# Row sums of an attention kernel folded onto half of the partitions, and their product with ones moved and halved

## The chip, the core and the metric

The kernel runs on one core of a Trainium2 chip. The metric is the device time of one execution in microseconds (us). Three runs of the kernel before took 2548.26, 2549.02 and 2549.62 us; the median, 2549.02, is the time that the change is measured against. The profiled execution took 2548.74 us, and its span in the profile is 2547.0 us, with a mean granted TensorE clock of 0.995.

## The reference

The input x has four images of 128 channels and 64 x 64 pixels. Layer 0 is a group norm, a 1x1 projection to q, k and v, attention with 4 heads of 32 channels over the 4096 pixels of an image, an output projection and a residual. Layer 1 is two 3x3 convolutions with quantized weights, each with a batch norm, and a residual. Only the attention matters here:

```python
q, k, v = jnp.split(qkv, 3, axis=1)            # (b, 128, 64, 64) each
q, k, v = (to_heads(q), to_heads(k), to_heads(v))   # (b, 4, 4096, 32)
attn = jnp.einsum('bhid,bhjd->bhij', q, k) * scale
attn = jax.nn.softmax(attn, axis=-1)
out = jnp.einsum('bhij,bhjd->bhid', attn, v)
...
out = jnp.einsum('oc,bchw->bohw', proj_w, out) + proj_b[None, :, None, None]
return x + out
```

The softmax's denominator is a sum of exponentials over all 4096 keys for each query and head. This row sum is what the change rearranges.

## The kernel before

**Blocks, steps and halves.** The attention is cut into 32 blocks (4 images x 8 groups of 512 queries), n = 0 to 31. A block runs over 32 key steps (kt) of 128 keys. For each step `scores` makes two matmul groups (`s<-q,k`, two heads each), and ScalarE (ACT) makes the exponentials `p` of both (128 keys on the partitions, 4 heads x 512 queries). `weights` then multiplies p by v into `acc`, in two halves of 256 queries, four matmuls for the four heads in four column bands of the array. There are 64 halves p = 0 to 63 in a block. `run_scores(3)` and `run_weights(3)` alternate, so that the work goes in rounds of three score halves and three weight halves.

**Row sums.** After the second half of a step, p is added into `rsum[n]` by VectorE (DVE, line 471). At the six steps of `MOVED` the addition is done by a DMA instead, into a second tile `msum[n]` (lines 464 and 466); each of these DMAs waits for the one before. Row sums are still split over the 128 partitions (keys), and that last sum is a matmul with a matrix of ones.

**What is left of a block is done in the next one.** `finish_parts(n)` gives closures, and `schedule` puts them at halves of block n+1 (`before[...]`):

- `merge` (half 3): GpSimd's DMA queue (POOL) adds msum into rsum.
- `sums` (line 498): the product with ones, `total`, in two groups of four matmuls of 256 columns, in PSUM tile `l`. Each head's sum comes out 32 times over, once on each partition of the head's band. The two groups come at the ends of two successive rounds, or of one.
- `evacuate`: ACT copies l to `ls`, 512 columns, directly after.
- `spread`, `invert`, `gather`: a DMA spreads the 4 x 512 sums over 128 partitions (`lq`), DVE makes reciprocals (`rq`), and two DMAs by way of a DRAM tile `rd` bring them back, repeated for the 32 partitions of each head (`rc`).
- `weigh` (line 537): DVE multiplies `av` (the copy of acc) by rc. `project` (line 317, `po`) multiplies it by the output weights, `store` adds bias and residual on DVE and writes the block to DRAM.

**Order.** The order is written out by hand and each engine runs its own queue in that order. `ends` lists the halves at which a round of this block ends; `at_half(p, f)` puts f behind weight half p, and `add(kt, f)` behind both halves of step kt. `visit(i, ...)` puts a product at ends[i] and its evacuation one half later. Projections of q, k and v for later blocks are visits too. The blocks in which two chunks of the next image are projected have `two` set: n = 3, 4, 5, 10, 11, 18 and 19. In these k, q and v of the first chunk are at ends[3], ends[7] and ends[9], and those of the second at ends[11], ends[13] and ends[15] (this code is not in the diff). A projection is evacuated by ACT (line 351, the high part) and then DVE (line 352, the low part), both reading the PSUM tile; v by DVE alone (line 371).

**Buffers.** PSUM has pool `pss` with three tiles of two banks for the scores, and pool `psa` with two tiles of one bank: acc, l, the projections and po all come from psa. Tiles p are in a pool of nine, rsum of two, msum, av, rc and ls of one each.

## Time and profile before

| engine | busy us | share of span |
|---|---|---|
| TensorE matmul (PE) | 2509.0 | 99% |
| TensorE weight load (PEld) | 1503.6 | 59% |
| VectorE (DVE) | 2137.2 | 84% |
| ScalarE (ACT) | 2087.4 | 82% |
| GpSimd (POOL) | 281.6 | 11% |

Attention takes most of the span: the first copy of a finished acc starts at 104.4 us and the last at 2234.1 us. The convolutions follow. The groups that the change touches, or that its work stands beside, are these (the mean is of one instruction):

| work | count | busy us | mean ns |
|---|---|---|---|
| PE, `l<-r,ones`, 256 columns | 496 | 36.7 | 379 |
| ACT, `ls<-l`, 512 columns | 32 | 18.8 | 588 |
| DVE, `r<-r,p`, the row-sum adds | 768 | 1758.2 | 2289 |
| DVE, `av<-av,rc` | 32 | 22.0 | 686 |
| POOL queue, `r<-rm` (merge), 1024 KB | 31 | 26.2 | 844 |
| POOL queue, `rm<-p` with addition, 1024 KB | 160 | 139.5 | 872 |

One matmul of this kernel leaves two records, so a group of four matmuls shows as eight. POOL's rows give the time to issue a DMA and not the transfer; from issue to landing merge takes 7.6 us in the median, and `rm<-p` 7.9 us (4.4 to 14.6). A timeline row gives the start in us from the span's start, the length of the merged run of instructions, engine, line, operation, output and inputs, and how many instructions are merged; in brackets is the time that the engine idled before it, and who ended that. The profile shows 5.7 us of waits of PE for `av<-av,rc` in all, and 4.1 us of waits of DVE for `rc<-rd`.

### The profile page before, as it was taken

What the parts mean: (1) busy time and instruction counts of PE and PEld (TensorE: products, weight loads), DVE (VectorE), ACT (ScalarE), POOL (GpSimd) and SP (SyncE); (2) the same over time, 40 slices, a digit from 0 to 9 for tenths busy, and PEclk for the clock granted to TensorE, in tenths of its full rate; (3) what the DMA queues carried; (4) which work ended last, traced back from release to release, by engine and by line L of the source; (5) the groups of instructions that cost most, each with busy time, mean ns of one, the idle gap of its engine ahead of it and who ended that gap; (6) DMA issues with size and microseconds to landing.
All of it is one profiled execution on the core that took longest, in us unless ns stands there. A gap on an engine that the chain in (4) does not pass through costs nothing.

```text
span 2547.0 us, 65043 instructions
## 1 busy us (share of the span) xinstructions
PE 2509.0 (99%) x28708; PEld 1503.6 (59%) x28708; DVE 2137.2 (84%) x1402; ACT 2087.4 (82%) x2278; POOL 281.6 (11%) x461
## 2 busy tenths in 40 slices
PE   9999999999999999999999999999999999999995
PEld 6555555555555555555555555555555555577774
DVE  6899888889988889889988888889999999954445
ACT  5999888999988999999988899989999999911224
POOL 2111111111011111110111111111000011000000
PEclk9999999999999999999999999999999999999998
DMA  6877667788757667797766666796666666745004
GB/s 193 192 185 169 168 173 181 171 203 182 184 132 190 170 152 169 164 231 164 173 163 172 157 166 158 191 203 150 149 138 144 146 145 149 150 90 160 1 1 166
DMA packets 148954, 403.86 MB, mean 159 GB/s; under 512 B 59416, under 2 KB 60184, under 8 KB 120120
## 3 DMA queue, kind: packets, MB, share of 16 engines
q0 software_dynamic: 45840, 280.39, 48.2%
q1 hardware_dynamic: 100952, 113.60, 16.9%
q10 hardware_dynamic: 1872, 5.64, 0.6%
q8 instruction: 227, 3.72, 0.6%
q14 instruction: 63, 0.52, 0.1%
HBM read 107.48 MB, written 56.42 MB: 64 GB/s over the span
## 4 chain that ended last, share of the span: by engine, by line
PE 92%; issue 3%; DMA 2%; DVE 1%; ACT 1%; ACTq 0%; POOL 0%; SPq 0%; POOLq 0%; DVEq 0%
PE s L442 41%; PE acc L456 36%; PE c L782 9%; DMA rm<-p 2%; PE l L488 1%; PE pq L317 1%; PE pk L317 1%; PE po L317 1%; PE pv L317 1%; DVE r L471 1%; ACT p L444 0%; ACT res L949 0%; DMA xh<-in_x_dram 0%; PE c_last L782 0%; DVE res L948 0%
## 5 line engine op out<-in xcount | busy, mean ns | idle before, releaser
L444 ACT ACTIVATE p<-s 128x1024 f32<-128x1024 f32 x2048 | 1950.5, 1032 | 201.6 <-PE s L442 154.5
L471 DVE TENSOR_TENSOR r<-r,p 128x2048 f32<-128x2048 f32 x768 | 1758.2, 2289 | 65.0 <-ACT p L444 14.5
L442 PE MATMUL s<-q,k 64*128 64x512 f32 x8192 | 1138.6, 409 | 1.7 <-ACT p L444 0.9
L456 PE MATMUL acc<-p,v 128*32 128x256 f32 x16384 | 1026.4, 383 | 0.0
L442 PEld LDWEIGHTS s<-q,k 64*128 64x128 f32 x8192 | 715.4, 184 | 410.3 <-issue 165.3
L456 PEld LDWEIGHTS acc<-p,v 128*32 128x32 f32 x16384 | 462.4, 109 | 483.7 <-issue 248.5
L466 POOL DMA_DIRECT2D rm<-p x160 | 139.5, 872 | 800.4 <-ACT p L444 535.5
L849 ACT COPY cv<-c 128x512 f32<-128x512 f32 x60 | 35.2, 586 | 200.1 <-DVE st L848 200.1
L782 PE MATMUL c<-hi,wq 128*128 128x512 f32 x540 | 139.1, 401 | 1.3 <-issue 1.3
L782 PE MATMUL c<-lo,wq 128*128 128x512 f32 x540 | 138.5, 400 | 0.0
L848 DVE BATCH_NORM_STATS2 st<-c 128x6 f32<-128x512 f32 x60 | 41.9, 699 | 103.9 <-PE c L782 83.4
L782 PEld LDWEIGHTS c<-hi,wq 128*128 128x128 f32 x540 | 101.2, 188 | 30.3 <-issue 2.1
L782 PEld LDWEIGHTS c<-lo,wq 128*128 128x128 f32 x540 | 101.6, 188 | 27.2
L352 DVE SCALAR_TENSOR_TENSOR kst<-pk,b,kst 128x512 fp32r<-128x512 f32 x32 | 24.0, 751 | 83.6 <-PE s L442 68.5
L469 DVE TENSOR_TENSOR r<-p,p 128x2048 f32<-128x2048 f32 x32 | 73.2, 2288 | 12.1 <-ACT p L444 11.1
L352 DVE SCALAR_TENSOR_TENSOR qst<-pq,b,qst 128x512 fp32r<-128x512 f32 x32 | 24.0, 751 | 58.2 <-PE s L442 47.3
L356 POOL DMA_DIRECT2D qd<-qst x31 | 23.6, 760 | 262.7 <-DVE qst L352 220.8
L492 POOL DMA_DIRECT2D r<-rm x31 | 26.2, 844 | 220.4 <-DMA rm<-p 95.1
L356 POOL DMA_DIRECT2D kd<-kst x27 | 20.0, 740 | 175.8 <-DVE kst L352 167.2
L488 PE MATMUL l<-r,ones 128*32 128x256 f32 (+1 forms) x504 | 37.7, 382 | 0.0
L464 POOL DMA_DIRECT2D rm<-p x32 | 17.8, 557 | 176.8 <-ACT p L444 93.4
L351 ACT ACTIVATE kst<-pk,b 128x512 fp32r<-128x512 f32 x32 | 22.3, 699 | 18.2 <-PE pk L317 18.2
(149 smaller groups left out, 739.3 us busy)
## 6 DMA issues: line engine op xcount, KB each, us to landing
rm<-p POOLq DMA_DIRECT2D x192, 1024.0 KB, 7.9
q<-qd SPq DMA_DIRECT2D x248, 128.0 KB
r<-rm POOLq DMA_DIRECT2D x31, 1024.0 KB, 7.6
x<-in_x_dram SPq DMA_DIRECT2D x86, 256.0 KB
k<-kd SPq DMA_DIRECT2D x124, 128.0 KB
qd<-qst POOLq DMA_DIRECT2D x31, 512.0 KB, 5.3
kd<-kst POOLq DMA_DIRECT2D x27, 512.0 KB, 4.8
y<-x POOLq DMA_DIRECT2D x32, 256.0 KB, 6.2
```

What stands on the lines that cost most here:

```text
L317: nc.tensor.matmul(out[cs, :], w[:, cs], x, start=True, stop=True)
L352: nc.vector.scalar_tensor_tensor(lo, ps[what], bias, t[:, 0, :], ALU.add, ALU.subtract)
L356: (nc.sync if start else nc.gpsimd).dma_start(out=dst[b, j].rearrange("s p n -> p s n"), in_=t)
L442: nc.tensor.matmul(s[:, i, :], k[r, half, c0 : c0 + P], q[r, half, part, :], start=(part == 0), stop=(part == 1))
L444: nc.scalar.activation(pts[step][:, 2 * half : 2 * half + 2, :], s, AF.Exp, scale=SCALE)
L456: nc.tensor.matmul(acc[n][h * D : (h + 1) * D, cs], v[:, kt % KB, h * D : (h + 1) * D], pt[:, h, cs], start=(kt == 0 and half == 0), stop= ...
L466: nc.gpsimd.dma_start(out=msum[n], in_=pt, accum_op=ALU.add)
L469: nc.vector.tensor_tensor(rsum[n], pts[step - 1], pt, ALU.add)
L471: nc.vector.tensor_tensor(rsum[n], rsum[n], pt, ALU.add)
L488: nc.tensor.matmul(t["l"][h * D : (h + 1) * D, cs], ones, r[:, h, cs], start=first, stop=end)
L782: nc.tensor.matmul(ps.rearrange("p (r w) -> p r w", w=W), w[:, tap, :], part[:, r0 + kh : r0 + kh + RB, kw : kw + W], start=(n == 0), stop ...
L848: nc.vector.bn_stats(st[:, b * NB + c, :], ps[:, j, :])
```

## The change

The product with ones shall need one group of four matmuls in place of two. A product with 32 columns per head puts the same sum on 32 partitions. The new matrix `pair` has ones in its upper half for 16 columns and in its lower half for the other 16, so that one matmul sums two heads, one lying on partitions 0 to 63 and the other on 64 to 127. For this the row sums have to lie on half of the partitions first. Two DMAs with addition do that (`fold`): heads 0 and 2 are added onto the lower partitions, heads 1 and 3 onto the upper. A DVE copy (`beside`) puts heads 1 and 3 of the upper partitions into the places of heads 0 and 2. Then four matmuls of 256 columns, for two pairs of heads and two halves of the queries, make all sums. The DMAs that follow read and write them in the new order, and gather is now two DMAs.

The chain gets longer by fold and beside, so its parts are put at other halves. sums is at ends[8] in every block, with evacuate one half later; before, the product was at ends[5], or at ends[6] and ends[7]. invert, gather and weigh are put farther along, and weigh stands two halves ahead of project, where it stood four ahead. The first of the MOVED steps is 6 in place of 4, to leave room for the fold in GpSimd's DMA queue; 9 and 14 become 10 and 15. The load of the next q is at step 17 in place of 14, and in block 1 one q projection goes from ends[8] to ends[6]. The last block's sums are made as before.

```diff
+    pair = const.tile([P, D], F32, name="pair")
+    nc.gpsimd.memset(pair, 0.0)
+    nc.gpsimd.memset(pair[: P // 2, : D // 2], 1.0)
+    nc.gpsimd.memset(pair[P // 2 :, D // 2 :], 1.0)
...
-    MOVED = (4, 9, 14, 19, 24, 28)
+    MOVED = (6, 10, 15, 19, 24, 28)
...
-        def total(r, first, end, cs=slice(0, FB)):
-            if "l" not in t:
-                t["l"] = psa.tile([P, FB], F32, name=f"l{n}", tag="a")
-            for h in range(HEADS):
-                nc.tensor.matmul(t["l"][h * D : (h + 1) * D, cs], ones, r[:, h, cs],
-                                 start=first, stop=end)
...
+        low, high = slice(0, P // 2), slice(P // 2, P)
+
+        def fold():
+            r = rsum[n]
+            nc.gpsimd.dma_start(out=r[low, 0::2, :], in_=r[high, 0::2, :], accum_op=ALU.add)
+            nc.gpsimd.dma_start(out=r[high, 1::2, :], in_=r[low, 1::2, :], accum_op=ALU.add)
+
+        def beside():
+            nc.vector.tensor_copy(rsum[n][high, 0::2, :], rsum[n][high, 1::2, :])
...
+        def sums():
+            l = psa.tile([P, FB], F32, name=f"l{n}", tag="a")
+            for c in range(4):
+                f, i = divmod(c, 2)
+                nc.tensor.matmul(l[c * D : (c + 1) * D, : FB // 2], pair,
+                                 rsum[n][:, 2 * i, f * FB // 2 : (f + 1) * FB // 2],
+                                 start=True, stop=True)
+            t["l"] = l
+
         def evacuate():
             t["ls"] = stage.tile([P, FB], F32, name=f"ls{n}", tag="ls")
-            nc.scalar.copy(t["ls"], t["l"])
-
-        def sums(i):
-            total(rsum[n], True, True, slice(i * FB // 2, (i + 1) * FB // 2))
-            if i == 1:
-                evacuate()
+            nc.scalar.copy(t["ls"][:, : FB // 2], t["l"][:, : FB // 2])
...
         def gather():
-            nc.sync.dma_start(out=rc, in_=t["rd"].unsqueeze(1).to_broadcast([HEADS, D, FB]))
+            for f in range(2):
+                nc.sync.dma_start(out=rc[:, f * FB // 2 : (f + 1) * FB // 2],
+                                  in_=t["rd"][f].unsqueeze(1).to_broadcast([HEADS, D, FB // 2]))
...
             add(1, before["merge"])
-            e = visit(5 if two or n == 1 else 6, lambda: before["sums"](0), lambda: before["sums"](1),
-                      split=not two and n != 1)
+            add(5, before["fold"])
+            add(9, before["beside"])
+            e = ends[8]
+            at_half(e, before["sums"])
+            at_half(e + 1, before["evacuate"])
             at_half(e + 2, before["spread"])
-            at_half(e + 8, before["invert"])
+            at_half(e + 10, before["invert"])
             at_half(e + 12, before["residual"])
-            at_half(e + 15, before["gather"])
-            at_half(ends[18] - 4, before["weigh"])
+            at_half(e + 17, before["gather"])
+            at_half(ends[18] - 2, before["weigh"])
             at_half(ends[18], before["project"])
             at_half(ends[18] + 2, before["store"])
         if n + 1 < len(blocks):
-            add(22 if n == 0 else 14, lambda: load_q(*blocks[n + 1]))
+            add(22 if n == 0 else 17, lambda: load_q(*blocks[n + 1]))
...
-            for i, j in zip((1, 3, 8, 10, 12, 14), range(2, NB)):
+            for i, j in zip((1, 3, 6, 10, 12, 14), range(2, NB)):
```

More of the change, by code (lines that the diff above doesn't have):

```diff
@@ L481, in copy @@
             nc.scalar.copy(av, acc[n])
-        def total(r, first, end, cs=slice(0, FB)):
-            if "l" not in t:
-                t["l"] = psa.tile([P, FB], F32, name=f"l{n}", tag="a")
-            for h in range(HEADS):
-                nc.tensor.matmul(t["l"][h * D : (h + 1) * D, cs], ones, r[:, h, cs],
-                                 start=first, stop=end)
         def merge():
             nc.gpsimd.dma_start(out=rsum[n], in_=msum[n], accum_op=ALU.add)
+        low, high = slice(0, P // 2), slice(P // 2, P)
[13 more added lines that the diff above has]
+            t["l"] = l
         def evacuate():
             t["ls"] = stage.tile([P, FB], F32, name=f"ls{n}", tag="ls")
-            nc.scalar.copy(t["ls"], t["l"])
-        def sums(i):
-            total(rsum[n], True, True, slice(i * FB // 2, (i + 1) * FB // 2))
-            if i == 1:
-                evacuate()
-        def sums_at_once():
-            total(msum[n], True, False)
-            total(rsum[n], False, True)
-            evacuate()
+            nc.scalar.copy(t["ls"][:, : FB // 2], t["l"][:, : FB // 2])
+        def sums_at_once():
+            l = psa.tile([P, FB], F32, name=f"l{n}", tag="a")
+            for r in (msum[n], rsum[n]):
+                for h in range(HEADS):
+                    nc.tensor.matmul(l[h * D : (h + 1) * D, :], ones, r[:, h, :],
+                                     start=(r is msum[n]), stop=(r is rsum[n]))
+            t["ls"] = stage.tile([P, FB], F32, name=f"ls{n}", tag="ls")
+            nc.scalar.copy(t["ls"], l)
             for j in range(4):
@@ L522, in spread @@
             t["lq"] = rpool.tile([P, FB // D], F32, name=f"lq{n}", tag="lq")
-            nc.sync.dma_start(out=t["lq"], in_=t["ls"][0:P:D, :])
+            nc.sync.dma_start(out=t["lq"], in_=t["ls"][0 : P : D // 2, : FB // 2])
         def invert():
@@ L527, in invert @@
             nc.vector.reciprocal(t["rq"], t["lq"])
-            t["rd"] = dram.tile([HEADS, FB], F32, name=f"rd{n}")
-            nc.sync.dma_start(out=t["rd"].rearrange("h (j c) -> (h j) c", c=FB // D), in_=t["rq"])
+            t["rd"] = dram.tile([2, HEADS, FB // 2], F32, name=f"rd{n}")
+            nc.sync.dma_start(out=t["rd"].rearrange("f h (j c) -> (f h j) c", c=FB // D), in_=t["rq"])
             nc.vector.tensor_tensor(worst, worst, t["lq"], ALU.add)
@@ L548, in store @@
             nc.gpsimd.dma_start(out=y0[b][:, qb * FB : (qb + 1) * FB], in_=t["x"])
-        return dict(copy=copy, merge=merge, sums=sums, sums_at_once=sums_at_once, bounds=bounds,
+        return dict(copy=copy, merge=merge, fold=fold, beside=beside, sums=sums,
+                    evacuate=evacuate, sums_at_once=sums_at_once, bounds=bounds,
                     spread=spread, invert=invert, gather=gather,
```

## The prediction

> **What bounds the kernel now.** I read the page first, then TensorE's timeline, then stretches of all engines around each instruction that the change moves.

> ```profile
> PE 2509.0 (99%) x28708; PEld 1503.6 (59%) x28708; DVE 2137.2 (84%) x1402; ACT 2087.4 (82%) x2278; POOL 281.6 (11%) x461
> ...
> PE 92%; issue 3%; DMA 2%; DVE 1%; ACT 1%; ACTq 0%; POOL 0%; SPq 0%; POOLq 0%; DVEq 0%
> ```

> TensorE (PE) is busy 99% and makes 92% of the chain of waits. So PE time taken out is gained, and a PE wait put in is paid. TensorE's timeline in a quiet stretch gives the unit (start us, length us):

> ```profile
> 1171.98 1.50 PE L456 MATMUL acc<-p,v 128*32 128x256 f32 x24
> 1173.30 0.61 PE L488 MATMUL l<-r,ones 128*32 128x256 f32 x8
> 1173.84 1.67 PE L442 MATMUL s<-q,k 64*128 64x512 f32 x12
> 1175.44 1.50 PE L456 MATMUL acc<-p,v 128*32 128x256 f32 x24
> 1176.88 1.67 PE L442 MATMUL s<-q,k 64*128 64x512 f32 x12
> 1178.48 1.50 PE L456 MATMUL acc<-p,v 128*32 128x256 f32 x24
> 1179.91 1.65 PE L442 MATMUL s<-q,k 64*128 64x512 f32 x12
> ```

> A round is three score halves and three weight halves: 1176.88 to 1179.91, 3.03 us. The round ahead of 1173.84 began at 1170.39 and held one l group of eight records: 3.45 us. **One l group costs 0.43 us**, not its 0.61 us of length, since its four column bands overlap their neighbours. Below, ends[i] is the end of round i of a block, where side work is put.

> [...] One psa bank holds acc for the block, so all side products share **one** bank, and each must be emptied before the next starts. [...] so one waiting group stops all scores behind it. The trace agrees:

> ```profile
> 1694.73 1.06 PE L317 MATMUL po<-av,wp 128*32 128x512 f32 x8 [1.84 <-DVE av L537]
> ```

> PE stood 1.84 us before po, and this round takes 5.9 us where a po round takes 3.88; nothing regains it. [...]

> **The change part by part.**

> *One l group for two.* Each of 31 blocks loses 0.43 us: **-13.3 us**. Evacuation of 256 columns instead of 512 (587 ns now) is ACT time hidden in the 0.17 us that ACT idles per round.

> *fold.* Two accumulating DMAs of 256 KB per block behind merge. Bounds for one are the two 256 KB rows of the DMA list (count, size, us from issue to landing):

> ```profile
> y<-x POOLq DMA_DIRECT2D x32, 256.0 KB, 6.2
> ...
> vd<-vst POOLq DMA_DIRECT2D x24, 256.0 KB, 3.8
> ```

> Both halves, issued one after the other (0.85 us each), should land 5 to 9 us after merge; I take 7. Merge lands 6 to 15 us into a block in the timelines, so fold lands at 13 to 22. GpSimd waits for merge ahead of the fold; behind it is the first moved p, now step 6 instead of 4, which already waited for that landing. Free.

> *beside.* A copy of 64x1024 f32 on DVE: between 0.68 us (the cast of 1188 columns takes 783 ns, scaled) and 1.07 us (the 2289 ns add of 2048, minus its fixed part, halved). [...] I take 0.7. Queued behind it on DVE are the row-sum adds, and behind those the PSUM evacuations that PE waits for. MOVED (6, 10, ...) puts one more 2.29 us add before step 9, but in blocks with a projection DVE now idles 1.4 to 5.8 us before kst or qst, which absorbs it. The add of step 8 now ends 17 to 25.5 us into a block; step 9's will end about then where it is absorbed, elsewhere (17 to 20) 2.3 us later; with 0.7 for the copy, beside ends at 18 to 26. PE arrives at ends[8] at 24 to 29, for each block at least 0.7 us later: no wait, except that copy and PE's gain bring DVE 1.1 us later against PE in the three blocks where it never idles (2, 9, 17), counted below.

> *sums at ends[8].* In the seven blocks with `two` (3, 4, 5, 10, 11, 18, 19) side products stand at ends[3], [7], [9]; the old sums sat at [5], two rounds from each. Now q, l and v take the one side bank in consecutive rounds. Block 4, all engines:

> ```profile
> 338.22 1.05 PE L317 MATMUL pq<-x,wn 128*32 128x256 f32 x16
> ...
> 342.23 1.66 PE L442 MATMUL s<-q,k 64*128 64x512 f32 x12
> 342.75 0.70 ACT L351 ACTIVATE qst<-pq,b 128x512 fp32r<-128x512 f32 x1
> ...
> 343.48 0.75 DVE L352 SCALAR_TENSOR_TENSOR qst<-pq,b,qst 128x512 fp32r<-128x512 f32 x1 [1.40 <-ACT qst L351]
> ```

> pq at 338.22; one round later, at 342.1, the new l would start. But ACT reads the bank at 342.75, behind three exponentials, and DVE until 344.23. PE stands **2.2 us**. evacuate too is put one half after its product now, so ACT does it behind the next three exponentials: 0.4 us after the following round ends, plus 0.37 us for 256 columns, plus 0.1 to release PE, where v wants to start 0.2 us before the round's end: **1.1 us**. 7 x 3.3 = **+23.1 us**. Elsewhere the neighbours of [8] are [6] and [10]: nothing.

> *Wider distances.* gather leaves 3 to 11 us later and still has 9 us or more ahead of weigh: free. weigh goes from four to two halves before project. One full step's add (kt 25 or 26) now stands ahead of it on DVE, and behind it is po on PE. Block 4 again, DVE's timeline, then PE's:

> ```profile
> 372.79 2.28 DVE L471 TENSOR_TENSOR r<-r,p 128x2048 f32<-128x2048 f32 x1
> 374.99 0.69 DVE L537 TENSOR_TENSOR av<-av,rc 128x512 f32<-128x512 f32 x1
> 375.60 4.68 DVE L471 TENSOR_TENSOR r<-r,p 128x2048 f32<-128x2048 f32 x2
> ```

> ```profile
> 375.85 1.04 PE L317 MATMUL po<-av,wp 128*32 128x512 f32 x8
> ```

> av ends at 375.68, po starts at 375.85, on time: slack 0.1 us. The add that follows starts at once, its p being ready, so it fits ahead of weigh without a gap: weigh 2.29 us later, PE waiting 2.29 minus slack. I read the slack of all 31 blocks from the same two timelines. The seven `two` blocks have 0.0 to 0.6 (2.9 together): 7 x 2.29 - 2.9 = 13.1. Block 1 has none: 2.3; blocks 9 and 31: 1.9 and 1.7; 7 and 16: 0.85 each; 6, 12 to 15, 20 to 22: about 0.54 each, 4.3; 2 and 17: 0.25 each; plus the 1.1 us in 2, 9 and 17. Others 15.8, together **+28.9 us**. Blocks 24 to 30 and 8 have over 2.3 us of slack; in 23 weigh is held by rc's DMA (3.74 us), taken as unchanged.

> *pair.* Four memsets of about 0.1 us at the start: +0.4 us at most. load_q at step 17 still has 15 steps; the q of block 1 at ends[6] stays two rounds from [8].

> Sum: 2549.0 - 13.3 + 23.1 + 28.9 + 0.4 = **2588 us**.

> **Rivals.**
> A, main (chance 0.50): both waits as worked out, 2588.
> B, the intended gain (0.14): bank and weigh hidden because DVE and ACT catch up: 2549.0 - 13.3 + 0.4 = 2536, faster. For it: DVE idles up to 5.8 us before some evacuations. Against: those idles are waits for PE itself, so DVE cannot be earlier there.
> C (0.17): the bank only; DVE, with fewer waits late in the block, does weigh in time: 2549.0 - 13.3 + 23.1 + 1 = 2560. For it: light blocks have that slack; against: block 4 has none.
> D (0.14): fold lands 10 us or more after merge under the load of the DMA queues (rm lands up to 14.6), DVE stands at beside and PE at sums: some 20 blocks x 1.3 us on top of A, 2614.
> E (0.05): bank waits halved and weigh hidden, within 0.2% of 2549.

> The range 2556 to 2612 leaves out B and E and, at the top, little over half of D's weight falls inside, so about 0.2 is outside. Faster 0.14 (B), same 0.05 (E), slower 0.81 (A, C, D).

> **What would show it.** An l group x8 once a block with rounds of 3.45 us confirms the gain. In block 4, PE idle about 2 us before l until DVE qst, and about 1 us before pv until ACT ls, confirm the bank; po rounds near 6 us instead of 3.88 in `two` blocks, with the wait on DVE av, confirm weigh. I am wrong if waits for DVE av stay near the 5.7 us of now, or if l waits on DVE's copy or on DMA fold in most blocks.

## The result, and the profile after

The changed kernel takes 2626.09 us (median of six runs, 2622.86 to 2634.7); six runs of the kernel before took 2548.81 us (2546.05 to 2550.02). The ratio is 1.0309, 95% interval 1.0292 to 1.0326: 77 us slower. The forecast was 2588 us, 39 us slower, so its direction held, half of the loss was missing in it, and the time lies above its range. The profile below is of the longest of the six runs (2634.7 us).

The page of the changed kernel: engines, then the chain of waits.

```profile
PE 2519.7 (96%) x28460; PEld 1499.1 (57%) x28460; DVE 2162.5 (82%) x1433; ACT 2075.9 (79%) x2278; POOL 344.5 (13%) x526
...
PE 36%; DMA 4%; issue 3%; DVE 3%; ACT 1%; SPq 1%; ACTq 0%; POOL 0%; DVEq 0%; POOLq 0%
```

TensorE (PE) was busy 99% and made 92% of the chain. The two chains can't be compared share by share: in the changed kernel the chain could be followed back only to 1361 us, so that its entries add up to 48% of the span, and PE makes 36 of the 48; the rest lies on DVE, the DMAs and SyncE's queue (SPq). PE has 248 matmul records fewer and yet 10.7 us more of busy time: some of its work ran at a lower clock (0.985 granted in the mean, 0.995 before). The waits of both kernels tell where it stands (engine, what it wanted to run, who ended the wait: us in all, times, longest). Before:

```profile
PE po L317 <- DVE av L537: 2.2, 2, 1.8
...
DVE av L537 <- DMA rc<-rd: 4.1, 3, 3.7
```

After:

```profile
PE po L321 <- DVE av L557: 58.1, 27, 9.3
DVE av L557 <- DMA rc<-rd: 20.5, 8, 8.8
PE l L508 <- DVE qst L356: 13.6, 7, 2.0
DVE av L557 <- DMA k<-kd: 8.7, 1, 8.7
PE pv L321 <- ACT ls L515: 5.3, 6, 0.9
```

The rows for l and pv are the shared bank, as forecast. The row for po was to hold about 29 us and holds 58.1 (the 5.7 us named for it ahead of the change are these 2.2 us and 3.5 us of the weight loads, PEld), and behind it stand 29.2 us in which DVE waits for a DMA at weigh (20.5 and 8.7). The second of these names the k load, but weigh reads av and rc only; k loads were issued just behind rc on the same queue.

Block 7 shows it. TensorE's timeline (start us, length us, what, and in brackets the idle time before it):

```profile
602.02 1.50 PE L460 MATMUL acc<-p,v 128*32 128x256 f32 x24
612.84 1.94 PE L321 MATMUL po<-av,wp 128*32 128x512 f32 x8 [9.31 <-DVE av L557]
614.70 2.86 PE L446 MATMUL s<-q,k 64*128 64x512 f32 x12
```

DVE's, and then that of SyncE's queue, which issues the loads:

```profile
612.09 0.69 DVE L557 TENSOR_TENSOR av<-av,rc 128x512 f32<-128x512 f32 x1 [8.66 <-DMA k<-kd]
```

```profile
585.16 5.54 SPq L426 DMA_DIRECT2D q<-qd  x8
590.81 4.57 SPq L415 DMA_DIRECT2D k<-kd  x4
...
598.61 1.10 SPq L553 DMA_DIRECT2D rc<-rd  x2
```

PE stood 9.31 us for weigh, weigh 8.66 us for rc, and rc had been issued at 598.61, after some 11 us of issues of q, k, v and x in the same queue. (By its semaphore in the trace rc's first DMA waited until the q load eight places ahead of it in this queue, issued at 589.53, had landed at 598.59, and the queue stood 2.15 us.) Weigh began 13.5 us after the issue. And po took 1.94 us instead of 1.04 and the next scores 2.86 instead of 1.66. Two stretches, the wait and po, tell why (length; busy us and instructions of PE, PEld, DVE, ACT, POOL; granted clock, DMA share, GB/s):

```profile
603.00:612.80 9.80, 0.52 (x12) 0.04 (x4) 1.14 (x3) 1.10 (x2) 0.83 (x1) 0.71 0.98 212
612.80:614.70 1.90, 1.86 (x8) 0.20 (x8) 1.90 (x1) 0.00 (x0) 0.00 (x0) 0.50 1.05 222
```

While rc was under way the DMA engines were busy throughout (share 0.98 in this wait, 1.13 at 600 to 603, 1.04 in the 10 us before). That is not new: in block 7 of the kernel before the share was 1.00 while rc was under way (569.3 to 582.9), and rc took as long, 13.5 us. But there it was issued 13.5 us before weigh was due, and here 4.8. Behind the wait the clock was 0.50. In the attention the kernel has nine stretches of half clock, 51 us together; the kernel before had none.

### The profile page after: what moved, and what is told of

Same layout as the page of the kernel before. It is cut to its first block, busy times and chain, and to the rows that moved or that the text cites. A ratio compares the mean times of both kernels' runs of the same rounds, so it can differ in the third digit from the quotient of the medians.

```text
span 2632.5 us, 64722 instructions
## 1 busy us (share of the span) xinstructions
PE 2519.7 (96%) x28460; PEld 1499.1 (57%) x28460; DVE 2162.5 (82%) x1433; ACT 2075.9 (79%) x2278; POOL 344.5 (13%) x526
## 3 DMA queue, kind: packets, MB, share of 16 engines
q1 hardware_dynamic: 105168, 113.60, 15.5%
## 5 line engine op out<-in xcount | busy, mean ns | idle before, releaser
L470 POOL DMA_DIRECT2D rm<-p x160 | 138.8, 867 | 875.4 <-ACT p L448 560.4
L321 PE MATMUL po<-av,wp 128*32 128x512 f32 x256 | 38.0, 669 | 58.1 <-DVE av L557 58.1
L488 POOL DMA_DIRECT2D r<-rm x31 | 26.1, 843 | 223.2 <-DMA rm<-p 70.6
L496 POOL DMA_DIRECT2D r<-r x31 | 31.3, 1010 | 121.8 <-DMA r<-rm 121.8
L321 PEld LDWEIGHTS po<-av,wp 128*32 128x32 f32 x256 | 5.6, 112 | 72.2 <-DVE av L557 71.1
L557 DVE TENSOR_TENSOR av<-av,rc 128x512 f32<-128x512 f32 x32 | 22.0, 688 | 29.2 <-DMA rc<-rd 20.5
## 6 DMA issues: line engine op xcount, KB each, us to landing
x<-in_x_dram SPq DMA_DIRECT2D x86, 256.0 KB
r<-r POOLq DMA_DIRECT2D x62, 256.0 KB, 5.1
```

The costliest lines, as they stand in the source:

```text
L321: nc.tensor.matmul(out[cs, :], w[:, cs], x, start=True, stop=True)
L470: nc.gpsimd.dma_start(out=msum[n], in_=pt, accum_op=ALU.add)
L496: nc.gpsimd.dma_start(out=r[low, 0::2, :], in_=r[high, 0::2, :], accum_op=ALU.add)
```

## The experiments

My theory after the result: gain 13 us, bank and order as forecast, and the missing 38 us from rc landing too late for weigh, with the half clock behind it. The rivals: that weigh's place alone is worth more than forecast; that fold is not free; that the forecast terms themselves are wrong. The runs of the kernel before on the same chips had medians of 2547.65 to 2548.9 us.

### e1: only weigh's place, in the kernel before

```diff
-            at_half(ends[18] - 4, before["weigh"])
+            at_half(ends[18] - 2, before["weigh"])
```

> The kernel before with one edit: weigh two halves ahead of project instead of four. Order theory (one more add on VectorE ahead of weigh makes TensorE wait before po): the waits of the prediction without the 3.3 us that belong to the copy, 2549 + 25 = 2574 us, po waits on DVE av near 26 us in all. DMA theory (weigh is late in the changed kernel because rc lands late, its place on VectorE matters little): 2549 us, po waits as before, 6 us.

Measured: 2575.68 us, ratio 1.0109 (1.0092 to 1.0126), +26.7 us. Waits of this kernel:

```profile
PE po L317 <- DVE av L537: 24.6, 22, 2.8
```

22 waits of up to 2.8 us, with hardly a DMA behind them (DVE waited 0.8 us for rc in all): one row-sum add ahead of weigh on DVE. The forecast term was 28.9, or 25.6 without the 3.3 us that belong to the copy. So this part was sized rightly, and what is missing is elsewhere.

### e2: weigh back at four halves, in the changed kernel

```diff
-            at_half(ends[18] - 2, before["weigh"])
+            at_half(ends[18] - 4, before["weigh"])
```

> The changed kernel with weigh back at four halves ahead of project. Order theory: the 27 us of order go, the waits for a late rc in blocks 7, 22 to 25 and some others stay: about 2599 us, and po waits remain only in blocks where weigh itself waits for rc. DMA theory: weigh starts when rc lands, wherever it stands: 2615 to 2626 us.

Measured: 2607.99 us, ratio 1.022 (1.0182 to 1.0258); 18 us better, between the two expectations. PE's wait for av fell from 58.1 to 35.4 us and from 27 times to 11; those of the seven `two` blocks went. DVE now stands longer for rc (20.5 us in 8 waits before this edit):

```profile
PE po L321 <- DVE av L557: 35.4, 11, 9.3
...
DVE av L557 <- DMA rc<-rd: 46.1, 16, 7.3
```

Where rc is late it doesn't matter where weigh stands: block 7 waited as long as before. So the cost of the order and that of a late rc overlap when only one is mended, and both are there.

### e3: the shorter distances of invert, gather and the q load

```diff
-            at_half(e + 10, before["invert"])
+            at_half(e + 8, before["invert"])
...
-            at_half(e + 17, before["gather"])
+            at_half(e + 15, before["gather"])
...
-            add(22 if n == 0 else 17, lambda: load_q(*blocks[n + 1]))
+            add(22 if n == 0 else 14, lambda: load_q(*blocks[n + 1]))
```

> The changed kernel with invert at e + 8, gather at e + 15 and the load of the next q at step 17 back to 14; weigh stays at two halves. If late rc (gather behind the q load and the k and v loads on the same queue) makes some 30 us of the excess, with the halved TensorE clock after the long waits: 2590 to 2600 us, and the two waits of 9 us in blocks 7 and 23 shrink to under 5. If rc is late because of the traffic of fold, little changes: 2615 or more.

Measured: 2616.88 us, ratio 1.0266 (1.0247 to 1.0286); only 9 us better, a miss: it lies where the rival was put. rc was issued 4 us earlier in blocks 7 and 23, and PE's waits there fell from 9.3 us to 3.7 and 4.0. But DVE came to invert before lq had landed (a wait of 4.4 us more is put down to the q load, issued behind it):

```profile
DVE rq L545 <- DMA lq<-ls: 7.6, 3, 3.8
```

Those waits at invert (3.8, 2.5 and 4.4 us in blocks 24, 27 and 30) push the adds and with them weigh, and block 30's po waited 5.0 us. The chain product, spread, invert, gather is too long for its place: two halves taken from one link are paid at the next.

### e4: without fold and beside

```diff
-            add(5, before["fold"])
-            add(9, before["beside"])
```

> The changed kernel without fold and beside (the two adding DMAs and the copy are left out, so the sums are those of partitions and heads not yet folded). If fold and beside are free, as predicted: 2620 to 2626 us, with the same waits for the bank and for av. If their traffic delays rc or their copy delays VectorE: 2600 us or less.

Measured: 2612.23 us, ratio 1.0246 (1.0229 to 1.0263), between the two expectations and 14 us better: fold is not free. PE's wait for av fell from 58.1 us:

```profile
PE po L321 <- DVE av L557: 42.4, 25, 4.6
```

In block 7 it fell from 9.3 to 4.3 and in block 23 from 9.3 to 2.3. In these two blocks rc was issued 2.9 and 2.7 us earlier against the time at which weigh was due, and weigh began 11.3 us after the issue, instead of 13.5 and 15.6: without fold's two DMAs of 256 KB per block both the loads ahead of rc and rc itself went faster there. Block 24 stayed late (4.5 us of wait, 3.6 with fold), and block 16, in which weigh had not waited for rc, now did (PE's wait 4.3 us instead of 1.9). So fold is a part of the lateness and not its only cause.

### e5: the side bank given room

In `two` blocks the projections stand at rounds 3, 6, 10 and 12, 14, 16, so none is next to the l at 8.

```diff
-dict(k=3, q=7, v=9) if i == 0 else dict(k=11, q=13, v=15)
+dict(k=3, q=6, v=10) if i == 0 else dict(k=12, q=14, v=16)
```

> The changed kernel with the projections of the seven two-chunk blocks put at ends[3], [6], [10] and [12], [14], [16], so that every neighbour of the sums is two rounds off. Bank theory: the waits of l on DVE qst and of pv on ACT ls go, 23 us by the prediction's sum, and a little more for the halved clock behind them: 2600 to 2604 us. Rival (PE would only wait later for DVE at the same total): 2620 or more.

Measured: 2601.55 us, ratio 1.0203 (1.0187 to 1.0219), 24.5 us better; the forecast term was 23.1. Block 4 in the changed kernel, PE's timeline:

```profile
352.01 0.64 PE L508 MATMUL l<-r,pair 128*32 128x256 f32 x8 [1.94 <-DVE qst L356]
...
356.53 1.08 PE L321 MATMUL pv<-wn,x 128*32 128x128 f32 x32 [0.85 <-ACT ls L515]
```

The same in e5:

```profile
346.45 1.67 PE L446 MATMUL s<-q,k 64*128 64x512 f32 x12
...
349.37 0.61 PE L508 MATMUL l<-r,pair 128*32 128x256 f32 x8
349.92 1.67 PE L446 MATMUL s<-q,k 64*128 64x512 f32 x12
```

Both waits are gone, and the round with l takes 3.47 us (346.45 to 349.92). PE's waits for av were still 56.8 us: bank and late rc are separate.

### e6: weigh doesn't read rc

```diff
-            nc.vector.tensor_tensor(av, av, rc, ALU.mult)
+            nc.vector.tensor_tensor(av, av, av, ALU.mult)
```

> The changed kernel in which weigh multiplies av by itself, so that nothing waits for rc (the reciprocals are made and brought back as before, but left out of the product). If late rc makes what the order of weigh does not explain: the 9 us waits in blocks 7 and 23 go, po waits fall to about the 29 us of the prediction, 2590 to 2597 us. If VectorE is late for another reason: 2615 or more.

Measured: 2597.35 us, ratio 1.0195 (1.0179 to 1.0211), 28.7 us better. All the DMAs still run; only nobody waits for rc. PE's wait for av:

```profile
PE po L321 <- DVE av L557: 28.4, 26, 2.8
```

This is e1's wait again (24.6 us, 22 times, 2.8 at the most): what is left is the order. The difference to 58.1 is the late rc.

### e7, e9, e10: what stays when the three costs are out

e7 is e6 with weigh at four halves and e5's spacing; e9 is e7 without fold and beside; e10 is e7 with the q load back at step 14.

> The changed kernel with all three causes taken away: weigh does not read rc (left out of the product), weigh at four halves, projections two rounds from the sums. If the list of causes is whole and fold and beside cost nothing by themselves: the gain alone, 2549 - 13.3 = 2536 us, no halved clock in the attention. If fold and beside cost TensorE time of their own: 2545 to 2560.

> The kernel with the three causes taken away (weigh does not read rc, weigh at four halves, projections two rounds from the sums), now also without fold and beside (left out, so the sums are not folded). It was 8 us over the gain alone, with scores waiting on p held by late adding DMAs around the change of image. If fold pushes that chain of DMAs: 2536 to 2538 us. If the moved steps and loads do it without fold: 2542 to 2545.

> The same kernel with the three causes taken away, with fold, and the load of the next q at step 14 as in the kernel before. If the q load at step 17, among the k and v loads of the next image, makes the adding DMAs late: 2537 to 2540 us. If fold makes them late: 2542 to 2546.

Measured: e7 2544.17 us, ratio 0.9982 (0.9976 to 0.9989); e9 2537.76, 0.9961 (0.9948 to 0.9973); e10 2547.55, 0.9996 (0.9988 to 1.0005). e7 lies between its two expectations and has one stretch of half clock in the attention (3.4 us), where none was expected. e9 met the first of its own. e10 missed both: it is 3.4 us slower than e7, not faster. So the q load at step 17 is not what holds e7, and fold with beside is: 6.4 us without any wait for rc. e7, waits:

```profile
ACT p L448 <- DMA rm<-p: 13.3, 7, 2.8
```

and e9:

```profile
ACT p L448 <- DMA rm<-p: 8.9, 5, 3.0
```

ACT can't write its exponentials because an adding DMA still reads the tile p. merge, two folds and six moved additions follow one another in GpSimd's queue, and where the loads of a new image fall in the same time, the chain runs behind: at the first change of image in e7 GpSimd stood 10.53 us before merge for a moved addition, and ACT 2.83 us for one before it could write p. In the kernel before this wait is 4.4 us. That fold slows the adding DMAs shows in their time from issue to landing, in the changed kernel and then in e9:

```profile
rm<-p POOLq DMA_DIRECT2D x192, 1024.0 KB, 8.5
```

```profile
rm<-p POOLq DMA_DIRECT2D x192, 1024.0 KB, 7.9
```

It is 8.4 in e7, and 7.9 again in e4 and in the kernel before.

### e8, e11, e12: can the whole change be made to pay?

e8 computes everything, with all mends at once: weigh at four halves, e5's spacing, evacuate and spread one half earlier, invert at e+8, gather at e+12, the q load at step 20, and the loads of k and v in the last block of an image partly two steps later.

```diff
-            at_half(e + 17, before["gather"])
-            at_half(ends[18] - 2, before["weigh"])
+            at_half(e + 12, before["gather"])
+            at_half(ends[18] - 4, before["weigh"])
...
-            add(22 if n == 0 else 17, lambda: load_q(*blocks[n + 1]))
+            add(22 if n == 0 else 20, lambda: load_q(*blocks[n + 1]))
```

> A whole kernel meant to keep the gain: weigh at four halves, projections two rounds from the sums, evacuate at e, spread e + 1, invert e + 8, gather e + 12, the next q loaded at step 20 (behind gather), and the k and v loads 4 to 6 of an image's last block two steps later (behind gather). If the causes are those named: 2536 to 2543 us, faster than before. If DMA lateness remains in blocks 7, 15, 23 and 24: 2545 to 2560.

Measured: 2553.66 us, ratio 1.0028 (1.0016 to 1.0039), a miss of the aim, within the range given for late DMAs. Late rc, bank and order are gone (PE's wait for av is 1.1 us in all), but the next block's q came too late, since its load is now issued among k and v. SyncE's queue and PE in block 7:

```profile
572.23 11.20 SPq L426 DMA_DIRECT2D q<-qd  x8
```

```profile
590.84 1.18 PE L446 MATMUL s<-q,k 64*128 64x512 f32 x3 [3.41 <-DMA q<-qd]
```

e11 puts the q load at step 14 in the last block of an image and at 17 elsewhere, and spreads k and v over later steps.

```diff
-            add(22 if n == 0 else 20, lambda: load_q(*blocks[n + 1]))
+            add(22 if n == 0 else 14 if qb == NB - 1 else 17, lambda: load_q(*blocks[n + 1]))
...
-                    add(4 * j + (1 if j < 4 else 3), lambda j=j: load_kv(b + 1, j))
+                    add((1, 5, 9, 19, 21, 24, 27)[j], lambda j=j: load_kv(b + 1, j))
```

> The whole kernel of the earlier attempt, with the q load at step 14 in the last block of an image and 17 elsewhere, and the k and v loads of the next image at steps 1, 5, 9, 19, 21, 24, 27, so that gather and q go ahead of them. The 3 us waits of scores for q in blocks 7 and 15 go: 2537 to 2545 us, against 2548. If k or v now come late in blocks 8, 16 and 24: 2550 or more.

Measured: 2555.18 us, ratio 1.0033 (1.0021 to 1.0045), also a miss. The wait for q is gone, PE waits for no k or v, and the wait for the adding DMAs is back, longer than in e7. Its waits:

```profile
DVE av L557 <- DMA rc<-rd: 16.9, 14, 3.4
ACT p L448 <- DMA rm<-p: 16.6, 6, 4.3
```

e12 is e11 with five moved additions per block instead of six, to shorten that chain.

```diff
-    MOVED = (6, 10, 15, 19, 24, 28)
+    MOVED = (7, 12, 17, 22, 27)
```

> The whole kernel of e11_best2 with five moved additions per block (steps 7, 12, 17, 22, 27) in place of six, so that the chain of adding DMAs holds merge, fold and five additions. Theory that this chain holds tiles p: the waits of ACT p for DMA rm (16.6 us in e11) and of scores for ACT p go away, and the time falls by 9 to 15 us from 2555.2 to 2540 to 2546, below the kernel before. Rival: DVE, with one more addition of 2.29 us per block, becomes late in the blocks in which it never idles (two-block projections, po): waits for DVE qst, kst or av take the place, 2552 or more.

Measured: 2589.2 us, ratio 1.0161 (1.0148 to 1.0175): the rival. The chain of waits of e12:

```profile
PE 31%; DVE 14%; DMA 6%; issue 5%; ACT 1%; SPq 0%; ACTq 0%; DVEq 0%; POOL 0%; POOLq 0%
```

and its waits:

```profile
PE po L321 <- DVE av L557: 30.8, 22, 5.8
```

ACT's wait for rm halved, to 8.1 us, as intended, but PE's wait for av is 30.8 us, where e11 has 4.3. DVE, at 86% busy, looks free and isn't: with 32 more adds on it weigh has no slack left. It waits for rc about as long as in e11 (18.9 us, 16.9 there), but now PE waits with it: 17 of the 30.8 us fall in blocks in which weigh waited for rc, the others behind the adds alone. (The chain goes back to 1081 us only; DVE makes 14 of the 57% of the span that it covers.) With six moved additions the DMA chain is late in some blocks, with five DVE is. No kernel with the whole computation and this change was faster than the kernel before; whether another order gets there wasn't tried.

## Why the forecast was half right

The account, from the runs:

| term | forecast us | measured us | from |
|---|---|---|---|
| one l group for two | -13.3 | -10.2 | e9 against before on its chips (2547.9), with waits for rm in it |
| bank in `two` blocks | +23.1 | +24.5 | changed kernel minus e5 |
| weigh behind one more add | +28.9 (25.6 without the copy's part) | +26.7 | e1 minus before |
| fold and beside | 0 | +6.4 | e7 minus e9 |
| gather late, rc waited for | 0 | +28.7 | changed kernel minus e6 |
| pair's memsets | +0.4 | not measured apart | |

2547.9 - 10.2 + 6.4 + 24.5 + 26.7 + 28.7 = 2624.0, against 2626.09 measured, so the account closes within 2.1 us. That is one comparison in fact: e6 minus e7 is 53.2 us, where bank and weigh make 51.2 together. The intervals of e1, e5 and e6 are each about 4 us to either side, so that it closes so well is in part luck. The terms come from different starting points, and e2 and e4 show that some overlap: out of the changed kernel fold takes 14 us with it, since rc is then less late.

**The gain.** The mechanism and the size held: one group of l per block, and its round takes 3.47 us where nothing waits. In e9 the 31 rounds with l are longer than plain rounds, which hold no side work, by 13.4 us together; in the kernel before the rounds with l were longer by 26.8. The 3 us by which e9 falls short of that are elsewhere: its plain rounds exceed their median of 3.027 us by 8.6 us in all, instead of 2.4. There PE waits for ACT's p, in e9 and then in the kernel before:

```profile
PE s L446 <- ACT p L448: 5.3, 11, 1.6
```

```profile
PE s L442 <- ACT p L444: 0.9, 5, 0.2
```

ACT's wait for rm is 8.9 us in e9 and 4.4 before; that this is what makes p late wasn't shown by a run.

**The bank.** Idle of 1.94 us before l until DVE's qst and 0.85 us before pv until ACT's ls, in 7 and 6 blocks, 18.9 us in all; forecast were 2.2 and 1.1 us of round, 23.1 us. The rounds with l and with pv are longer than undisturbed ones by 22.9 us, since a stretch of half clock follows the wait for l in block 10. The price read from ACT's and DVE's place in block 4's timeline was right in mechanism and near in size.

**weigh.** 22 waits in e1, and in the changed kernel 1.8 to 2.0 us of excess in the po rounds of all seven `two` blocks (13.2 us, forecast 13.1). That this was read block by block from DVE's slack made it hold.

**beside.** 691 ns against 0.7 us. Of the two values scaled from the trace, 0.68 and 1.07 us, the lower was the right one; that it would be was my estimate. No l waited for it in the changed kernel.

**The step that failed: "gather leaves 3 to 11 us later and still has 9 us or more ahead of weigh: free".** Both halves of it were wrong, and waiting for rc cost 28.7 us (e6). In blocks 7, 23, 24 and 25 rc was issued 4.8, 6.8, 6.9 and 8.7 us before weigh was due, since gather stands in SyncE's queue behind the loads of q, k, v and x (in block 24 it waited for rd to land, 8.8 us after its issue). And 9 us would not have been enough: in the nine blocks in which weigh waited for rc, 10.5 to 15.6 us passed from its issue to weigh. The trace of the kernel before had said so, in block 23 (SyncE's queue, then DVE):

```profile
1666.63 9.35 SPq L422 DMA_DIRECT2D q<-qd  x8
...
1679.66 0.55 SPq L534 DMA_DIRECT2D rc<-rd  x1
```

```profile
1693.98 0.69 DVE L537 TENSOR_TENSOR av<-av,rc 128x512 f32<-128x512 f32 x1 [3.74 <-DMA rc<-rd]
```

14.3 us from issue to weigh, with 9.35 us of q issues ahead in the queue. I read the 3.74 and put this block down "as unchanged", where it was one of three blocks that showed the price of the step; in the other two, 8 and 29, weigh waited 0.2 us at 12.1 and 12.3 us from the issue. Leads of 10 to 15 us were needed. In block 23 the wait of po went from 1.8 to 9.3 us. In block 7, where so small a transfer took so long, the DMA share was 0.98 to 1.13, with GpSimd's additions and SyncE's loads at once; that this load is the cause is an inference of mine that no run shows alone.

A part of the same step stood at nothing without a reason: gather had become two DMAs. The semaphores in the traces tell when rc landed, counted from the first issue. One DMA of 256 KB took 7.6 us in the median of 31 blocks in the kernel before (5.3 to 14.3) and 7.9 in e1; the two of 128 KB took 11.3 in the changed kernel (6.5 to 15.5), 11.2 without fold (e4), and 10.3 to 12.5 in all other runs. So fold is not what raised this median. That the second DMA did is likely and not shown, as gather also moved in all these runs; no run left it as one DMA. In blocks 7 and 23, where the longest waits were, rc had taken 13.5 and 14.3 us already in the kernel before, and there the lost lead decides.

None of the prediction's signs of error could have told of this: waits for av did not stay near 5.7 us, and l waited for neither the copy nor fold. (Its chance outside the range is also summed too low: B and E with about half of D make 0.26, not 0.2.)

**The second: fold "free".** It was right where it looked: fold was in time for sums. It was not asked what 512 KB more per block do to other transfers. They make rc later in blocks 7 and 23 (13.5 and 15.6 us from its issue to weigh, 11.3 in both without fold, e4), and even with nobody waiting for rc they hold p (ACT waits 13.3 us for rm in e7 and 8.9 in e9), with the adding DMAs landing after 8.5 us in the median, where it was 7.9.

**The half clock.** It wasn't in the forecast. 51 us at half clock are inside the terms above, 41 of them in blocks in which weigh waited for rc: plain rounds exceed their median of 3.027 us by 14.5 us in all, and by 2.4 before. Rival D had 2614 from a late fold, nearer to the measured time than the main forecast; its cause (DVE at beside) didn't come about.

## What to carry to other kernels

A small DMA that an engine must wait for is priced from its issue in its queue's real order (loads in front of it included) to its landing under the load of that stage, and one instruction in the trace of before that waits for it tells that price (14.3 us in block 23 here); read its lead in every block as one reads an engine's slack. Extra DMA traffic need not be free where the share of the DMA engines is near 1 (0.98 to 1.13 in block 7), even if its own result is early (fold with beside cost 6.4 us between e7 and e9): ask whose transfers it delays. And when a chain is lengthened, mending one link hands the wait to the next (invert, q, p, DVE here); PE waits of some us can cost more than their length, where the clock is halved behind them (behind the 9.31 us in block 7 po took 1.94 us instead of 1.04).

## What the runs showed of the hardware

```profile
791.40:794.80 3.40, 3.40 (x32) 1.52 (x32) 3.26 (x3) 2.97 (x4) 0.00 (x0) 0.51 0.40 154
```

it (third column from the right) is 0.51 for one unit, with PE busy throughout. In e1 none of 22 waits, up to 2.8 us, brought a half clock in the attention (the profiled run was granted 0.995 in the mean, as the kernel before).

In the changed kernel a wait of the same length went both ways: block 4's 1.94 us before l at 352.01 had no half clock behind it (1.00 from 352 to 360). What differs is how much idle time of PE falls into one unit. The nine stretches begin whole multiples of 3.4133 us apart (to 0.01 us), so the attention can be cut into such units. Nine of the units at full clock hold 1.75 us or more of PE's idle time, and just these nine are followed by half clock; the next one holds 1.71. Block 10's wait lies with 1.88 us in one unit; block 4's falls across two, with 1.04 and 0.90. Of the 15 units at half clock the nine behind which the clock came back hold no idle time of PE, and the other six 0.67 us or more. The units were cut for the changed kernel alone, so for the waits of e1 this is not shown. So a wait of about 2 us can cost its own length or some 1.7 us more, by where it falls (an estimate: half of the clock over one unit of 3.41 us).
